# Graph attention with layer norm: the group's loads issued in pieces, slot by slot, two groups ahead

## The chip, the cores and the metric

The kernel runs on one core of a Trainium2 chip. The metric is device time in microseconds (us) of one execution; lower is better. A core has five engines that run their own lists of instructions and wait for each other by semaphores: TensorE (PE in the profile; PEld are its weight loads), VectorE (DVE), ScalarE (ACT), GpSimd (POOL) and SyncE (SP). SP computes nothing here: it issues plain loads and stores. POOL issues the indirect gathers. All transfers run on the core's 16 DMA engines.

## What is computed

One graph layer on 6250 nodes of 128 numbers and 206250 edges, sorted by receiver, then a residual and a layer norm:

```python
w_ij = silu(edge_feats @ rad_W1 + rad_b1) @ rad_W2 + rad_b2
w_ij = w_ij + (silu(chi_scalar @ sph_W1 + sph_b1) @ sph_W2 + sph_b2)
q_i = (x @ Wq)[receivers]          # 8 heads of 16
k_j = (x @ Wk)[senders]
v_j = (x @ Wv)[senders]
alpha = (q_i * w_ij * k_j).sum(-1) / sqrt(16) * cutoffs
out = segment_sum(alpha * v_j, receivers) / 16
x = layernorm(x + out)
```

Everything is float32. Each edge brings 32 + 32 features, a weight, a sender and a receiver.

## The kernel before

*Tiles.* 128 edges are a tile, 4 tiles (512 edges) a quad, 4 quads a group. There are 101 groups and 403 quads. A group's quads are taken in the order 0, 2, 1, 3; the place in this order is called the slot, so slots 0, 1, 2, 3 hold quads 0, 2, 1, 3. Quads of slots 0 and 1, and those of slots 2 and 3, form pairs for the features' first matmul.

*Start.* The first stage computes the keys and values of all nodes, stores them in a table in memory (kv_tab), turns the receivers into positions within a window of 32 rows per quad (rel, stored in memory as rel_lin), and makes tables of window starts (qb_i per quad, gb_i per group).

*The loop* runs over groups g and slots. The order of the work is written by hand (a manual schedule): each engine's list is the order in which the program calls. In a slot for quad q:

- `gathers` (L132): four indirect gathers on POOL, each 128 rows of 1 KB of kv_tab, for the quad 14 slots ahead, into a ring of 16 buffers named kv. A buffer comes free when VectorE's msg (L415) has read it.
- `weigh` (L375): two matmuls (L379), then ScalarE adds the bias and writes w (L381).
- `turn_back` (L395) of the quad before: four transposes of u into pu (L399).
- `take_q` (L384): receivers' queries spread to the edges by a matmul with hotT (L388).
- in slots 0 and 2 `hidden` (L359) for the next pair: four matmuls from feats (L367), each into one of four PSUM buffers named ph, and four silus on ScalarE (L372).
- in slot 1 `sum_group` of group g-2 (two matmuls, L446 and L448, and a copy to tot on ScalarE, L450) and `turn_q` of group g+1 (a transpose of xq, L336, and a copy, L338); in slot 3 `make_q` of group g+1.
- `sum_quads` of group g-1: matmuls that add messages per receiver (L425); two tiles' worth in slot 1, one each in slots 2 and 3.
- `scores` (m at L404, L406, L407), `multiply` (u at L393) and `messages` (msg at L415) on VectorE. m needs pu from TensorE and the gathered kv.
- in slot 2 the transposed one-hots hotT of group g+1 (L350, from relb) and `statistics` of group g-2, which needs xw; after every fourth group it also normalizes four groups' rows and stores them (L479).

*SP's list* in this order for group g: after slot 0, `load_q(g + 1)` (four loads of 32 rows of x at a start that SP reads from qb_i, 16 KB each, L158, tile xq), `load_xw(g - 1)` (64 KB, L455) and `load_rel(g + 1)` (four loads of 32 KB that copy a quad's receivers to 32 rows each, L150, tile relb); after slot 1, `load_feats(g + 2)` (one load of 128 rows of 4 KB, 512 KB, L140); in slot 2 of every fourth group four stores of 64 KB. SP works through its list as fast as waits allow: a load waits until its buffer is free (xq, relb, feats and xw have two buffers each), a store until ScalarE has written its rows. In feats, rows 0 to 63 hold quads 0 and 1 side by side, rows 64 to 127 quads 2 and 3.

Before the loop come, in this order, `turn_q(0)`, `make_q(0)`, the one-hots of group 0, `load_feats(1)`, `load_rel(1)` and `hidden` for the first pair.

Of the kernel before, what the change touches and what calls it, by code (L numbers as in the profile page):

```python
# [12 lines left out]
F32 = mybir.dt.float32  # L13
BF16 = mybir.dt.bfloat16
# [8 lines left out]
P = 128  # L23
N = 6250
D = 128
HEADS = 8
HD = D // HEADS
R = 32
# [3 lines left out]
NQ = GT // QT  # L32
NG = math.ceil(E / (P * GT))
NT = NG * GT
EG = P * GT
EQ = P * QT
# [15 lines left out]
def gnn_kernel(ctx, tc, x, src, dst, weight, edges, rad_W1, rad_b1, rad_W2, rad_b2,  # L52
# [12 lines left out]
    nc = tc.nc  # L65
# [13 lines left out]
    w1 = const.tile([P, D], F32, name="w1")  # L79
# [20 lines left out]
    gp = ctx.enter_context(tc.tile_pool(name="group", bufs=2))  # L100
# [15 lines left out]
    def start_of(table, i, last):  # L116
        return nc.values_load(table[:1, i:i + 1], engines=(SP,), min_val=0, max_val=last,
                              skip_runtime_bounds_check_because="the table is clamped to it")
# [10 lines left out]
    feats_of, relb_of, act_of, kv_of, hot_of, hotT_of, xq_of, q_of, msg_of = ({} for _ in range(9))  # L129
    po_of, part_of, to_of, tot_of, xw_of, y0_of, u_of = ({} for _ in range(7))  # L130

    def gathers(q):  # L132
        kv = quad_of("kv", RING, 2 * D)
        for t in range(QT):
            gather(kv[:, t, :], kv_tab, src_i[:, q * QT + t:q * QT + t + 1])
        kv_of[q] = kv

    def load_feats(g):
        feats_of[g] = gp.tile([P, EG // 2], F32, name="feats")
        nc.sync.dma_start(feats_of[g], edges[g])  # L140

    def quads_in(g):
        return min(NQ, QUADS - g * NQ)

    def load_rel(g):

        relb_of[g] = gp.tile([P, EQ], BF16, name="relb")
        for j in range(NQ):
            t = g * GT + j * QT
            nc.sync.dma_start(relb_of[g][j * W:(j + 1) * W, :],  # L150
                              rel_lin[t:t + QT, :].rearrange("t e -> (t e)").partition_broadcast(W))

    def load_q(g):

        xq_of[g] = gp.tile([P, D], F32, name="xq")
        for j in range(quads_in(g)):
            r = start_of(qb_i, g * NQ + j, N - W)
            nc.sync.dma_start(xq_of[g][j * W:(j + 1) * W, :], x[ds(r, W), :])  # L158

# [172 lines left out]
    with tc.tile_pool(name="ps", bufs=1, space=PSUM) as pp:  # L332
        def turn_q(g):
            n = quads_in(g) * W
            pt = pp.tile([P, EQ], F32, name="ph", bufs=4)
            nc.tensor.transpose(pt[:, :n], xq_of[g][:n, :], ident[:n, :n])  # L336
            xq_of[g] = gp.tile([P, P], F32, name="xqT")
            nc.scalar.activation(xq_of[g][:, :n], pt[:, :n], AF.Copy)  # L338
# [20 lines left out]
        def hidden(pair):  # L359

            for q in pair:
                g, j = divmod(q, NQ)
                r0, c0 = 2 * R * (j // 2), EQ * (j % 2)
                for i in range(2):
                    ph = pp.tile([P, EQ], F32, name="ph", bufs=4)
                    r = slice(r0 + i * R, r0 + (i + 1) * R)
                    nc.tensor.matmul(ph, w1[r, :], feats_of[g][r, c0:c0 + EQ], start=True, stop=True)  # L367
                    act_of[q, i] = ph
            for q in pair:
                for i in range(2):  # L370
                    act = ep.tile([P, EQ], F32, name="act", bufs=8)
                    nc.scalar.activation(act, act_of[q, i], AF.Silu, bias=b1[:, i:i + 1])  # L372
                    act_of[q, i] = act

        def weigh(q):  # L375

            pw = pp.tile([P, EQ], F32, name="ph", bufs=4)
            for i in range(2):
                nc.tensor.matmul(pw, w2[:, i, :], act_of[q, i], start=(i == 0), stop=(i == 1))  # L379
            w = ep.tile([P, EQ], F32, name="w")  # L380
            nc.scalar.activation(w, pw, AF.Identity, bias=bsum)  # L381
            return w

        def take_q(q):  # L384
            g, j = divmod(q, NQ)
            b = slice(j * W, (j + 1) * W)
            pq = pp.tile([P, EQ], F32, name="pq")
            nc.tensor.matmul(pq, q_of[g][b, :], hotT_of[g][b, :], start=True, stop=True)  # L388
            return pq
# [5 lines left out]
        def turn_back(q):  # L395

            pu = pp.tile([P, QT, D], F32, name="pu")
            for t in range(QT):
                nc.tensor.transpose(pu[:, t, :], u_of[q][:, t * P:(t + 1) * P], ident)  # L399
            return pu  # L400
# [37 lines left out]
        def part_sums(g):  # L438
            n = quads_in(g) * W
            part_of[g] = gp.tile([P, D], F32, name="part")  # L440
            nc.scalar.activation(part_of[g][:n, :], po_of[g][:n, :], AF.Copy)  # L441

        def sum_group(g):
            n, part, to = quads_in(g) * W, part_of[g], to_of[g]
            ph = pp.tile([P, EQ], F32, name="ph", bufs=4)
            nc.tensor.matmul(ph[:, :D], to[:n, 0, :], part[:n, :], start=True, stop=(g == 0))  # L446
            if g:
                nc.tensor.matmul(ph[:, :D], to[:, 1, :], tot_of[g - 1], start=False, stop=True)  # L448
            tot_of[g] = gp.tile([P, D], F32, name="tot")
            nc.scalar.activation(tot_of[g], ph[:, :D], AF.Copy)  # L450

        def load_xw(g):
            r = start_of(gb_i, g, N - P)
            xw_of[g] = gp.tile([P, D], F32, name="xw")
            nc.sync.dma_start(xw_of[g], x[ds(r, P), :])  # L455
# [40 lines left out]
        def verdict():  # L496

            pe = pp.tile([P, D], F32, name="po")
            nc.tensor.matmul(pe[:1, :8], ones[:, :1], ends, start=True, stop=True)
            found = gp.tile([1, 1], F32, name="found")  # L500
            nc.vector.tensor_reduce(found, pe[:1, :8], AX.X, OP.add)
            nc.vector.tensor_scalar(general, found, 0.0, None, op0=OP.is_gt)
# [3 lines left out]
        one_hots_T(0)  # L506
        one_hots(0)
        load_feats(1)
        load_rel(1)
        hidden(pairs[0])  # L510
        before = None
        for g in range(NG):
            last = g == NG - 1
            for slot, j in enumerate((0, 2, 1, 3)):
                q = g * NQ + j
                i = g * NQ + slot
                if q >= QUADS:
                    continue
                if i + AHEAD < len(order):
                    gathers(order[i + AHEAD])  # L520
                if slot == 0 and 2 <= g:
                    part_sums(g - 2)
                    if g == CHECK + len(checks) + 1:
                        verdict()
                w = weigh(q)
                if before is not None:
                    pu = turn_back(before)
                pq = take_q(q)
                if slot % 2 == 0:
                    u = 2 * g + slot // 2 + 1  # L530
                    if u < len(pairs):
                        hidden(pairs[u])
                if slot == 1 and 2 <= g:
                    sum_group(g - 2)
                if slot == 1 and g + 1 < NG:
                    turn_q(g + 1)
                if slot == 3:
                    make_q(g + 1)
                if 1 <= g:
                    for t in ((), (0, 1), (2, 3))[slot] if last else ((), (0, 1), (2,), (3,))[slot]:  # L540
                        sum_quads(g - 1, t)
                if before is not None:
                    alpha = scores(before, pu)
                multiply(q, pq, w)
                if before is not None:
                    messages(before, alpha)
                before = q
                if slot == 0:
                    if g + 1 < NG:
                        load_q(g + 1)  # L550
                    if 1 <= g:
                        load_xw(g - 1)
                        if g + 1 < NG:
                            load_rel(g + 1)
                if slot == 1:
                    if g + 2 < NG:
                        load_feats(g + 2)
                    if 1 <= g:
                        place(g - 1)
                    if last:  # L560
                        place(g)
                        load_xw(g)
                if slot == 2 and g + 1 < NG:
                    one_hots_T(g + 1)
                if slot == 2 and 2 <= g:
                    statistics(g - 2)
                if slot == 3:
                    one_hots(g + 1)
                    if CHECK <= g < CHECK + len(checks):
                        checks[g - CHECK]()  # L570
        g = NG - 1
# [170 lines left out]
```

## Time and profile before

| what | value |
|---|---|
| three runs | 2854.62, 2856.44, 2858.70 us |
| median | 2856.44 us |
| the profiled execution | 2843.93 us |
| its span, first to last instruction | 2841.9 us |
| mean granted TensorE clock | 0.847 |
| busy: PE, DVE, ACT, POOL | 81%, 50%, 35%, 54% of the span |
| gathers of kv on POOL | 1580 x 948 ns |
| moved by DMA | 310.42 MB, mean 109 GB/s |

The page cuts the span into 40 equal slices; a digit is the busy share of a slice in tenths (9 is 90% or more). PEclk is the clock that TensorE was granted, in tenths of full speed. A line of a group of instructions reads: line of the code, engine, operation, output and inputs, shapes, count, busy time in us and mean ns of one, then the idle time of the engine just before them and what ended it ("remote" is a releaser that the profile doesn't know, "issue" none that it shows). In a timeline the columns are start, us, engine, line, operation, and in brackets the idle time before it with its releaser. In a table of stretches each engine has its busy share of the stretch and, in brackets, the number of instructions.

### The profile page before, as it was taken

To read this page: it belongs to the slowest core of one execution; us is meant where nothing else is said; L and a number is where in the kernel's file an instruction comes from. 1 tells how busy PE (TensorE), PEld (TensorE's weight loads), DVE (VectorE), ACT (ScalarE), POOL (GpSimd) and SP (SyncE) were. 2 spreads that over 40 slices of the span, in tenths; PEclk is the share of its full clock that TensorE was granted. 3 is DMA by queue.
4 is the path that set the end of the run, shared out by engine and by line. 5 is a ranking of instruction groups with operands and counts; after the bars stand their busy time and mean duration, and the time that the engine had idled before them with its cause. 6 is when DMAs were issued, how large, how long until landed. Compare 5 with 4: busy or idle time off the path is not lost. (4 is left out here: it accounts for less than half of the span.)

```text
span 2841.9 us, 32012 instructions
## 1 busy us (share of the span) xinstructions
PE 2310.3 (81%) x9843; PEld 1023.9 (36%) x9843; DVE 1412.9 (50%) x2874; ACT 1000.3 (35%) x1826; POOL 1530.0 (54%) x1620
## 2 busy tenths in 40 slices
PE   5578878878887888888888888888888878788887
PEld 4333333333333333333333333333333333333333
DVE  3244554555554544545454454554544545455456
ACT  1233333333332433333333343333333333333334
POOL 4455555555555555555555555555555555555540
PEclk7788988888788887878888888888888888888889
DMA  5433333333333333333333333333334333333330
GB/s 175 133 111 97 118 105 114 113 102 111 118 105 111 102 118 102 110 111 104 110 107 112 116 98 110 119 102 120 108 99 119 103 106 116 107 112 113 108 99 26
DMA packets 166844, 310.42 MB, mean 109 GB/s; under 512 B 46530, under 2 KB 99212, under 8 KB 166668
## 3 DMA queue, kind: packets, MB, share of 16 engines
q0 software_dynamic: 76864, 209.29, 25.4%
q1 hardware_dynamic: 88316, 98.64, 10.5%
q8 instruction: 79, 1.29, 0.2%
q14 instruction: 97, 0.79, 0.1%
q10 hardware_dynamic: 1488, 0.40, 0.1%
HBM read 294.70 MB, written 13.46 MB: 108 GB/s over the span
## 5 line engine op out<-in xcount | busy, mean ns | idle before, releaser
L113 POOL DMA_INDIRECT kv<-kv_tab,src_i x1580 | 1498.5, 948 | 1217.7 <-DVE msg L415 748.5
L379 PE MATMUL ph<-act,w 128*128 128x512 f32 x1612 | 961.9, 726 | 95.8 <-ACT act L372 73.5
L404 DVE TENSOR_TENSOR m<-pu,kv 128x512 f32<-128x512 f32 x403 | 278.7, 691 | 1240.3 <-remote 434.1
L367 PE MATMUL ph<-feats,w 32*128 32x512 f32 x1612 | 626.3, 726 | 259.6 <-ACT w L381 198.4
L372 ACT ACTIVATE act<-ph,b 128x512 f32<-128x512 f32 x806 | 500.4, 688 | 317.6 <-PE ph L367 222.8
L381 ACT ACTIVATE w<-ph,bsum 128x512 f32<-128x512 f32 x403 | 276.9, 687 | 758.4 <-PE ph L379 286.7
L379 PEld LDWEIGHTS ph<-act,w 128*128 128x128 f32 x1612 | 325.1, 224 | 524.0 <-issue 367.4
L388 PE MATMUL pq<-hotT,q 32*128 32x512 f32 x806 | 475.8, 671 | 2.6 <-issue 2.6
L367 PEld LDWEIGHTS ph<-feats,w 32*128 32x128 f32 x1612 | 202.8, 206 | 454.9 <-ACT w L381 269.6
L399 PEld LDWEIGHTS pu<-ident,u 128*128 128x128 f32 x1612 | 215.1, 151 | 350.9 <-issue 200.6
L399 PE MATMUL pu<-ident,u 128*128 128x128 f32 x1612 | 259.5, 286 | 86.5 <-DVE u L393 83.7
L393 DVE TENSOR_TENSOR u<-pq,w 128x512 f32<-128x512 f32 x403 | 274.8, 682 | 55.1 <-PE ph L367 39.6
L406 DVE TENSOR_REDUCE side<-m 128x32 f32<-128x512 f32 x403 | 280.1, 695 | 13.7
L415 DVE TENSOR_TENSOR msg<-kv,side 128x512 f32<-128x512 f32 x403 | 273.0, 677 | 0.0
L425 PE MATMUL po<-msg,hot 128*32 128x128 f32 x3224 | 173.1, 312 | 2.9 <-ACT part L441 2.9
L450 ACT ACTIVATE tot<-ph 128x128 f32<-128x128 f32 x101 | 28.0, 277 | 399.3 <-remote 138.2
L388 PEld LDWEIGHTS pq<-hotT,q 32*128 32x128 f32 x806 | 123.2, 191 | 76.4 <-issue 76.4
L425 PEld LDWEIGHTS po<-msg,hot 128*32 128x32 f32 x3224 | 77.6, 117 | 154.2 <-issue 136.7
L407 DVE TENSOR_TENSOR side<-side,scale 128x32 f32<-128x32 f32 x403 | 80.4, 199 | 13.8
L346 ACT ACTIVATE q<-ph 128x128 f32<-128x128 f32 (+1 forms) x101 | 28.0, 277 | 144.8 <-issue 66.1
L350 DVE TENSOR_TENSOR hotT<-relb,side 128x512 f32<-128x512 bf16 x101 | 68.8, 681 | 0.0
L355 DVE TENSOR_TENSOR hot<-rel,side 128x512 f32<-128x512 f32 x101 | 68.8, 681 | 0.0
(83 smaller groups left out, 813.2 us busy)
## 6 DMA issues: line engine op xcount, KB each, us to landing
feats<-in_edges SPq DMA_DIRECT2D x101, 512.0 KB
kv<-kv_tab,src_i POOLq DMA_INDIRECT x1580
relb<-rel_lin SPq DMA_DIRECT2D x404, 32.0 KB
xw<-in_x SPq DMA_DIRECT2D x101, 64.0 KB
out<-y SPq DMA_DIRECT2D x101, 64.0 KB
xq<-in_x SPq DMA_DIRECT2D x403, 16.0 KB
kv_tab<-kv SPq DMA_DIRECT2D x12, 512.0 KB
act<-in_x SPq DMA_DIRECT2D x12, 256.0 KB
```

The source lines that it names most:

```text
L113: nc.gpsimd.indirect_dma_start(out=o, out_offset=None, in_=table, in_offset=bass.IndirectOffsetOnAxis(ap=index, axis=0))
L367: nc.tensor.matmul(ph, w1[r, :], feats_of[g][r, c0:c0 + EQ], start=True, stop=True)
L372: nc.scalar.activation(act, act_of[q, i], AF.Silu, bias=b1[:, i:i + 1])
L379: nc.tensor.matmul(pw, w2[:, i, :], act_of[q, i], start=(i == 0), stop=(i == 1))
L381: nc.scalar.activation(w, pw, AF.Identity, bias=bsum)
L388: nc.tensor.matmul(pq, q_of[g][b, :], hotT_of[g][b, :], start=True, stop=True)
L393: nc.vector.tensor_tensor(u_of[q], pq, w, op=OP.mult)
L399: nc.tensor.transpose(pu[:, t, :], u_of[q][:, t * P:(t + 1) * P], ident)
L404: nc.vector.tensor_tensor(m, pu, kv_of[q][:, :, :D], op=OP.mult)
L406: nc.vector.tensor_reduce(alpha, m.rearrange("p t (h e) -> p t h e", e=HD), AX.X, OP.add)
L415: nc.vector.tensor_tensor(msg_of[q].rearrange("p t (h e) -> p t h e", e=HD), kv_of[q][:, :, D:].rearrange("p t (h e) -> p t h e", e=HD), a ...
L425: nc.tensor.matmul(po_of[g][j * W:(j + 1) * W, :], hot_of[g][:, j * QT + t, :], msg_of[g * NQ + j][:, t, :], start=(t == 0), stop=(t == QT ...
```

## The change

The features' tile becomes two tiles, feats0 (quads 0 and 2) and feats1 (quads 1 and 3), each 128 rows of 2 KB with two buffers of its own, and each is loaded in two pieces of 64 rows and 128 KB: pieces 0 and 1 into feats0, 2 and 3 into feats1. After every slot of group g SP is given one piece of the features of group g+2, one load of 32 rows of x (xq) for it, and one quad's receivers (relb), where before it had four of a kind in one place: xq and relb were loaded one group ahead after slot 0, the features two groups ahead after slot 1. Tiles xq and relb get three buffers instead of two. `load_xw(g - 1)` stays after slot 0, now behind these three. `load_q(1)` moves ahead of the loop. The bytes loaded and all instructions of TensorE, VectorE, ScalarE and POOL, and their order, stay as they are.

```diff
--- before.py
+++ after.py
@@ -135,25 +135,34 @@
             gather(kv[:, t, :], kv_tab, src_i[:, q * QT + t:q * QT + t + 1])
         kv_of[q] = kv
 
-    def load_feats(g):
-        feats_of[g] = gp.tile([P, EG // 2], F32, name="feats")
-        nc.sync.dma_start(feats_of[g], edges[g])
+    def load_feats(g, parts=range(4)):
+
+
+        for k in parts:
+            i, b = k // 2, slice(k % 2 * 2 * R, (k % 2 + 1) * 2 * R)
+            if k % 2 == 0:
+                feats_of[g, i] = gp.tile([P, EQ], F32, name=f"feats{i}")
+            nc.sync.dma_start(feats_of[g, i][b, :], edges[g, b, i * EQ:(i + 1) * EQ])
 
     def quads_in(g):
         return min(NQ, QUADS - g * NQ)
 
-    def load_rel(g):
-
-        relb_of[g] = gp.tile([P, EQ], BF16, name="relb")
-        for j in range(NQ):
+    def load_rel(g, quads=range(NQ)):
+
+        for j in quads:
+            if j == 0:
+                relb_of[g] = gp.tile([P, EQ], BF16, name="relb", bufs=3)
             t = g * GT + j * QT
             nc.sync.dma_start(relb_of[g][j * W:(j + 1) * W, :],
                               rel_lin[t:t + QT, :].rearrange("t e -> (t e)").partition_broadcast(W))
 
-    def load_q(g):
-
-        xq_of[g] = gp.tile([P, D], F32, name="xq")
-        for j in range(quads_in(g)):
+    def load_q(g, quads=range(NQ)):
+
+        for j in quads:
+            if j >= quads_in(g):
+                continue
+            if j == 0:
+                xq_of[g] = gp.tile([P, D], F32, name="xq", bufs=3)
             r = start_of(qb_i, g * NQ + j, N - W)
             nc.sync.dma_start(xq_of[g][j * W:(j + 1) * W, :], x[ds(r, W), :])
 
@@ -360,11 +369,11 @@
 
             for q in pair:
                 g, j = divmod(q, NQ)
-                r0, c0 = 2 * R * (j // 2), EQ * (j % 2)
+                r0 = 2 * R * (j // 2)
                 for i in range(2):
                     ph = pp.tile([P, EQ], F32, name="ph", bufs=4)
                     r = slice(r0 + i * R, r0 + (i + 1) * R)
-                    nc.tensor.matmul(ph, w1[r, :], feats_of[g][r, c0:c0 + EQ], start=True, stop=True)
+                    nc.tensor.matmul(ph, w1[r, :], feats_of[g, j % 2][r, :], start=True, stop=True)
                     act_of[q, i] = ph
             for q in pair:
                 for i in range(2):
@@ -507,6 +516,7 @@
         one_hots(0)
         load_feats(1)
         load_rel(1)
+        load_q(1)
         hidden(pairs[0])
         before = None
         for g in range(NG):
@@ -545,16 +555,13 @@
                 if before is not None:
                     messages(before, alpha)
                 before = q
-                if slot == 0:
-                    if g + 1 < NG:
-                        load_q(g + 1)
-                    if 1 <= g:
-                        load_xw(g - 1)
-                        if g + 1 < NG:
-                            load_rel(g + 1)
+                if g + 2 < NG:
+                    load_feats(g + 2, (slot,))
+                    load_q(g + 2, (slot,))
+                    load_rel(g + 2, (slot,))
+                if slot == 0 and 1 <= g:
+                    load_xw(g - 1)
                 if slot == 1:
-                    if g + 2 < NG:
-                        load_feats(g + 2)
                     if 1 <= g:
                         place(g - 1)
                     if last:
```

## The prediction

> **What bounds the kernel now.** I read the page first (busy rows, clock row, costliest groups), then stretches of single groups, then the timeline of one group, then the waits of SP's queue and of TensorE.
>
> The page, parts 2 and 5:
>
> ```profile
> PE   5578878878887888888888888888888878788887
> POOL 4455555555555555555555555555555555555540
> PEclk7788988888788887878888888888888888888889
> ...
> L113 POOL DMA_INDIRECT kv<-kv_tab,src_i x1580 | 1498.5, 948 | 1217.7 <-DVE msg L415 748.5
> ...
> L404 DVE TENSOR_TENSOR m<-pu,kv 128x512 f32<-128x512 f32 x403 | 278.7, 691 | 1240.3 <-remote 434.1
> ```
>
> No engine is full: PE is at 81%, its granted clock at 0.85, and both POOL (waiting for VectorE's msg to free a kv buffer, 748.5 us) and VectorE (before m, 1240.3 us) stand idle for long. Four single groups by stretch, three with gathers and one after the last gather (columns: us, busy share with count of PE, PEld, DVE, ACT, POOL, then granted clock, DMA share, GB/s):
>
> ```profile
> 1405.10:1432.70 27.60, 22.99 (x96) 9.67 (x96) 13.47 (x27) 8.70 (x17) 15.17 (x16) 0.88 0.35 103
> ...
> 1487.80:1514.20 26.40, 23.21 (x96) 10.09 (x95) 13.44 (x28) 8.37 (x16) 14.94 (x16) 0.87 0.45 127
> 1189.80:1216.30 26.50, 22.21 (x96) 9.69 (x96) 13.36 (x27) 8.48 (x16) 14.80 (x17) 0.82 0.36 111
> ...
> 2779.80:2798.90 19.10, 18.08 (x96) 8.59 (x97) 13.49 (x28) 8.86 (x17) 0.00 (x0) 1.00 0.18 53
> ```
>
> The same 96 matmul records take 19.1 us without gathers and 26.4 to 27.6 us with them. From the starts of m, groups 0 to 96 average 27.08 us; sixteen gathers, one per 1.25 us, are 20.0 us of it. The rest is in the timeline of one such group:
>
> ```profile
> 1511.10 0.36 SPq L140 DMA_DIRECT2D feats<-in_edges  x1
> ...
> 1515.44 0.39 PE L448 MATMUL ph<-tot,to 128*128 128x128 f32 x2
> ...
> 1518.27 0.60 PE L399 MATMUL pu<-ident,u 128*128 128x128 f32 x4
> ...
> 1521.78 0.94 POOL L113 DMA_INDIRECT kv<-kv_tab,src_i  x1 [0.30 <-issue]
> 1523.70 0.28 ACT L450 ACTIVATE tot<-ph 128x128 f32<-128x128 f32 x1 [9.27 <-remote]
> ...
> 1525.35 0.69 DVE L404 TENSOR_TENSOR m<-pu,kv 128x512 f32<-128x512 f32 x1 [7.59 <-remote]
> ...
> 1528.46 0.94 POOL L113 DMA_INDIRECT kv<-kv_tab,src_i  x1 [5.73 <-DVE msg L415]
> ```
>
> The transposes that m waits for end at 1518.87, yet m starts 6.5 us later, and ScalarE's tot stands as long, 2.6 us after POOL's last gather ended (1522.73). POOL then idles 5.7 us until msg frees a buffer. I call this a stall: about one per group, and nearly every stall over 3 us ends only when POOL has run out of free buffers. Its cause is not named by the profile ("remote"). After it the granted clock reads 0.50 for some 6 us, and the next slot takes 7.0 us instead of 4.2. So a group costs POOL's 20 us plus POOL's idle time around one such run-out.
>
> SP's queue and TensorE, waits:
>
> ```profile
> SPq L140 <- PE ph L367: 493.8, 63, 18.2
> SPq L455 <- DVE st L465: 463.9, 66, 16.5
> SPq L479 <- ACT y L476: 443.6, 25, 21.7
> ...
> PE ph L336 <- issue: 21.5, 10, 7.3
> ...
> PE ph L336 <- DMA xq<-in_x: 7.0, 6, 1.9
> ```
>
> SP waits 1400 us on compute: its loads are early. The one place where compute waits for a load is L336, which needs xq.
>
> **The change part by part.** The order of the instructions on PE, VectorE, ScalarE and POOL is the same before and after; only SP's list differs.
>
> *Features in four pieces.* Three issues more per group; one takes 0.36 us (0.357 median of the 101), so 1.1 us per group on SP, which waits 1400/101 = 14 us per group: cost 0, and no compute engine waits for feats (no wait of L367 on a DMA is listed). If that cover were gone, 1.1 us per group would be 107 us. Transfer: the whole 512 KB showed as DMA share 0.76, 0.85, 1.00 in three 1 us slices (up to 391 GB/s); a 128 KB piece is bounded by that rate (0.33 us) and by the relb load's row (32 KB per 0.45 us of issue, so 1.8 us). Either lands far inside the more than one group by which it is early: 0.
>
> [...]
>
> *When the pieces go.* The first two (buffer feats0) wait for hidden of slot 2 a group earlier, the other two for hidden of slot 0; so SP sends two bursts per group, not four. Slot 0: from 512 + 4x16 KB to 256 + 32 + 64 = 352 KB. Slot 2: from xw 64 + relb 128 = 192 KB to 256 + 32 + 64 + 64 = 416 KB. Does this move the stall? In groups after the four output stores feats goes in slot 2 instead (1496.93 in the group that starts at 1487.8): that group is 26.4 us and the stall is still there, m starting at 1498.65 after 7.55 us idle. So the burst in slot 0 isn't what makes it. But its place does change: around 1190 m's gaps within a group are 5.1, 9.5, 3.4, 8.6 us, where the commoner form is 11.1, 7.0, 4.2, 5.1. Groups with a first gap of 10.8 us or more: 49, mean 28.1 us; the other 48: 26.0 us. They partly pay for each other (a short group follows a long one), so the whole 2.1 us is no gain per group. Any four groups in a row take 103.7 to 114.1 us, most of them 105.4 to 111.0, against the mean of 108.3: per group -0.7 to +0.7 us, over 97 groups -71 to +65 us. These are the bounds for a new phase of loads. I take -10 us, near the middle, a little below since the largest burst shrinks.
>
> *xq two groups ahead.* Gain: at most the waits of L336. Of 21.5 us, 7.3 lie at 112 us in the start; 14.2 + 7.0 = 21.2 us remain. But in the group at 1487.8 PE waited 1.5 us there and m came 9.88 us after L448 started, against 9.91 in the group of 1511.10, which did not wait: the stall hides it. Bounds -21 and 0; I take -5, nearer that pair.
>
> *relb per quad, two groups ahead.* hotT shows no idle time for relb, before or after: 0. Late next is nothing that SP loads: xw stays in its place behind a feature piece, and y's add waits for no DMA in the profile; the output stores now stand ahead of the fourth piece instead of the next xq, and this piece has a group to spare.
>
> *Start.* Features 0 in four issues put 1.1 us ahead of the last two kv_tab stores, and features 1 and xq 1 go out earlier than group 0 needs them. Bounds 0 and +2; I take +1.
>
> Sum: -10 - 5 + 1 = -14 us. The profiled execution took 2843.9 us (span 2841.9 and 2.0 around it) and becomes about 2830; the runs' median stands 12.5 us above it, so 2856.4 becomes 2842.
>
> **The rivals.**
> 1. *A second stall per group (slower).* The burst in slot 2 grows from 192 to 416 KB and lands while POOL has just restarted. For it: around 1190 a stall of 5 us begins within 1 us of the xw and relb loads of slot 2. Against it: in the group at 1487.8 feats, xq, xw and relb all went in slot 2, and the next gaps were 6.2, 4.2, 5.1 us. Price: POOL's idle 5.7 us per added stall. It decides from the fourth extra stall on (14 us of gain used up at the third); in every tenth group 9 x 5.7 = 51 us, 2893; in every fifth 19 x 5.7 = 108 us, 2950.
> 2. *The loads settle into the better pattern everywhere (faster).* For it: four-group stretches at 105.4 us exist in the run. Against it: they never last. 71 us: 2785.
> 3. *The stall goes (much faster).* Then 20.0 us of POOL remain per group, 97 x 7.08 = 687 us: 2170. Against it: the stall is there in groups without feats in slot 0, and the gathers stay.
> 4. *The change does nothing that counts.* The loads were early before: 2856.
>
> **How the numbers follow.** The likeliest case (0.42) gives 2842, its own range 2815 to 2865. Rival 1: 0.33; rival 2: 0.15; rival 3: 0.03; rival 4: 0.07. The likeliest, 2842 within bounds of -71 and +65 us, gives 2770 to 2907; the upper end moves to 2920, to take in most of the first rival, and 0.1 lies above it. About 0.08 lies below 2770. This kernel's measurement tells 0.2% from no change, 5.7 us. Faster: 0.30 of the likeliest, 0.15 and 0.03: 0.48. Same: 0.05 of the likeliest and 0.06 of rival 4: 0.11. Slower: 0.33, 0.07 and 0.01: 0.41.
>
> **What would show it.** Right: L336 without waits for xq; feats as four issues in two pairs per group; stretches near 27 us with sixteen gathers; POOL's wait for msg near 748 us. Wrong: POOL's wait for msg well above 850 us (more stalls) or below 650; a wait of L367 on a feature DMA; single groups beyond 28 us as the rule. The number fails if the stall answers to SP's bursts in a way that no group of this run shows.

## The result, and the profile after

The changed kernel took 2862.83 us (median of 20 runs, 2847.96 to 2870.84) beside 2855.20 us (20 runs, 2848.66 to 2861.37) of the kernel before on the same chip: ratio 1.0019, 95% interval 1.0010 to 1.0028. That is 0.2% slower (0.27% between the medians), on the edge of what a measurement of this kernel can tell from no change. The forecast was 0.5% faster. On another chip the same change was later 2.0% faster; this decides how the forecast is to be read and is told below.

The profiled execution of the changed kernel took 2868.33 us, near the top of its runs, and that of before 2843.93 us, below all 20 runs of the comparison. The two profiles lie 24 us apart where the medians lie 7.6 us apart, so small differences between them are to be read with care.

The page of the changed kernel, busy tenths and the two groups that were shown of before:

```profile
PE   5678887888878788888788888887888878788788
POOL 4455555555555555555555555555555555555540
PEclk7678878889888898898888988988889889888899
...
L113 POOL DMA_INDIRECT kv<-kv_tab,src_i x1580 | 1493.6, 945 | 1247.1 <-DVE msg L424 784.2
...
L413 DVE TENSOR_TENSOR m<-pu,kv 128x512 f32<-128x512 f32 x403 | 278.5, 691 | 1273.8 <-remote 637.6
```

Nothing became full or empty. POOL's wait for msg is 784.2 us (748.5 before), m's wait that ends on an unknown releaser 637.6 us (434.1). Four groups by stretch (us; busy and count of PE, PEld, DVE, ACT, POOL; granted clock; DMA share; GB/s), the last without gathers:

```profile
1201.40:1228.60 27.20, 22.30 (x96) 9.53 (x96) 13.44 (x27) 8.64 (x17) 15.12 (x16) 0.87 0.36 108
1419.80:1447.30 27.50, 22.76 (x96) 9.75 (x97) 13.45 (x28) 8.92 (x17) 15.30 (x17) 0.88 0.36 107
1502.50:1529.00 26.50, 21.94 (x95) 9.43 (x95) 13.48 (x28) 8.46 (x16) 14.34 (x16) 0.87 0.43 125
2804.50:2823.10 18.60, 17.82 (x96) 8.45 (x97) 13.44 (x28) 8.67 (x17) 0.00 (x0) 1.00 0.15 46
```

The stall is still there, in the same place: in 93 of the 97 groups (87 before) VectorE stands idle and m starts over 3 us after the last transpose has ended. The timeline of a group that starts at 1228.64:

```profile
1232.73 0.60 PE L408 MATMUL pu<-ident,u 128*128 128x128 f32 x4
...
1236.21 0.95 POOL L113 DMA_INDIRECT kv<-kv_tab,src_i  x1 [0.30 <-issue]
1239.63 0.69 ACT L390 ACTIVATE w<-ph,bsum 128x512 f32<-128x512 f32 x1 [4.79 <-remote]
1239.69 0.69 DVE L413 TENSOR_TENSOR m<-pu,kv 128x512 f32<-128x512 f32 x1 [7.69 <-remote]
...
1242.79 0.94 POOL L113 DMA_INDIRECT kv<-kv_tab,src_i  x1 [5.63 <-DVE msg L424]
```

The transposes end at 1233.33, m starts 6.4 us later, after POOL's last gather has ended (1237.16), and POOL then waits 5.63 us for msg. From the starts of m, groups 0 to 96 average 27.33 us (27.08 before). The form with gaps of 11.0, 7.0, 4.2 and 5.1 us between the m's of a group, which was the commoner one before, now holds two thirds of the groups: 66 of 97 have a first gap of 10.8 us or more (49 before), and so have 37 of the 43 groups from 27 to 69. 0.26 us x 97 = 25 us is the whole distance of the two spans.

The waits of SP's queue and of TensorE:

```profile
SPq L145 <- PE ph L376: 979.2, 124, 12.9
SPq L488 <- ACT y L485: 407.0, 24, 18.0
...
SPq L464 <- DVE st L474: 36.1, 3, 18.0
```

```profile
PE ph L345 <- issue: 5.7, 1, 5.7
```

The features' pieces wait for hidden in two pairs per group (124 waits). The transpose of xq (L345) waits once, in the start, and nowhere in the loop.

### The profile page after: what moved, and what is told of

Same layout as the page of the kernel before. It is cut to its first block, busy times and chain, and to the rows that moved or that the text cites. A ratio compares the mean times of both kernels' runs of the same rounds, so it can differ in the third digit from the quotient of the medians.

```text
span 2866.2 us, 32442 instructions
## 1 busy us (share of the span) xinstructions
PE 2307.5 (81%) x9843; PEld 1018.6 (36%) x9843; DVE 1412.1 (49%) x2874; ACT 1001.0 (35%) x1826; POOL 1524.9 (53%) x1620
## 3 DMA queue, kind: packets, MB, share of 16 engines
q0 software_dynamic: 76864, 209.29, 25.2%
## 4 chain that ended last, share of the span: by engine, by line
PE 61%; another core or an unknown queue 17%; issue 8%; ACT 6%; POOL 4%; DVE 3%; DMA 0%; DVEq 0%; SPq 0%; POOLq 0%; ACTq 0%
PE ph L388 25%; PE ph L376 11%; PE pq L397 10%; PE pu L408 5%; POOL kv L113 4%; PE po L434 4%; ACT act L381 3%; ACT w L390 2%; PE ph L353 1%; PE ph L455 1%; PE pk L228 1%; DVE side L415 1%; DVE m L413 1%; PE ph L457 1%
## 5 line engine op out<-in xcount | busy, mean ns | idle before, releaser
L113 POOL DMA_INDIRECT kv<-kv_tab,src_i x1580 | 1493.6, 945 | 1247.1 <-DVE msg L424 784.2
L388 PE MATMUL ph<-act,w 128*128 128x512 f32 x1612 | 937.9, 711 | 95.0 <-ACT act L381 88.0
L376 PE MATMUL ph<-feats,w 32*128 32x512 f32 x1612 | 664.3, 706 | 365.9 <-ACT w L390 288.0
L413 DVE TENSOR_TENSOR m<-pu,kv 128x512 f32<-128x512 f32 x403 | 278.5, 691 | 1273.8 <-remote 637.6
L397 PE MATMUL pq<-hotT,q 32*128 32x512 f32 x806 | 461.7, 653 | 0.3 <-issue 0.3
L376 PEld LDWEIGHTS ph<-feats,w 32*128 32x128 f32 x1612 | 210.3, 201 | 583.4 <-ACT w L390 376.3
L408 PEld LDWEIGHTS pu<-ident,u 128*128 128x128 f32 x1612 | 208.0, 146 | 284.4 <-issue 190.0
L408 PE MATMUL pu<-ident,u 128*128 128x128 f32 x1612 | 249.6, 279 | 38.9 <-DVE u L402 38.9
L359 DVE TENSOR_TENSOR hotT<-relb,side 128x512 f32<-128x512 bf16 x101 | 68.5, 678 | 0.0
L364 DVE TENSOR_TENSOR hot<-rel,side 128x512 f32<-128x512 f32 x101 | 68.5, 678 | 0.0
```

Source lines behind the costliest of these rows:

```text
L113: nc.gpsimd.indirect_dma_start(out=o, out_offset=None, in_=table, in_offset=bass.IndirectOffsetOnAxis(ap=index, axis=0))
L376: nc.tensor.matmul(ph, w1[r, :], feats_of[g, j % 2][r, :], start=True, stop=True)
L413: nc.vector.tensor_tensor(m, pu, kv_of[q][:, :, :D], op=OP.mult)
```

## Experiments on the chip of the first kind

Four theories stood against each other. A: the stall belongs to the gathers and the compute; what SP loads has next to no price. B: loads of 64 rows or their phase cost something. C: the place of xq and relb in SP's list is what counts. D: SP's loads make the stall. Four altered kernels were measured beside before, which had a median of 2850.88 us there (23 runs).

**The features alone.** xq and relb stay as before.

```diff
                 before = q
+                if g + 2 < NG:
+                    load_feats(g + 2, (slot,))
                 if slot == 0:
...
                 if slot == 1:
-                    if g + 2 < NG:
-                        load_feats(g + 2)
                     if 1 <= g:
```

(and load_feats and hidden as in the change)

> Kernel before with one part of the change: the features in four pieces of 64 rows, one issued after each slot, two groups ahead; xq and relb loaded as before. Theory A (the stall of each group belongs to gathers and compute; SP's loads don't shape it, and the change only alters how often a group falls into the commoner form with the long first gap): within 0.3% of before, groups near 27.1 to 27.3 us, the count of groups with a first gap of 10.8 us or more anywhere between 49 and 66. Theory B (the small loss comes from the pieces of 64 rows, which occupy the DMA engines longer): slower than before by 0.2% or more, like the whole change. Theory C (the loss comes from where the loads of receivers and x stand): same as before within 0.1%.

Measured: 2897.79 us, ratio 1.0169 (1.0127 to 1.0212). Its waits at TensorE:

```profile
PE ph L339 <- DMA xq<-in_x: 47.3, 13, 6.6
...
PE ph L339 <- issue: 18.0, 6, 6.4
```

Theory A (within 0.3%) and theory C (within 0.1%) missed this; B (0.2% or more) holds by the number, but not by its cause. All the waits in the loop lie in the group after the four output stores, so in every fourth. The timeline before the longest of them:

```profile
1506.99 7.94 SPq L482 DMA_DIRECT2D out<-y  x4
1514.98 1.12 SPq L143 DMA_DIRECT2D feats<-in_edges  x2
1517.16 7.87 SPq L161 DMA_DIRECT2D xq<-in_x  x4
...
1525.88 0.45 PE L339 MATMUL ph<-ident,xq 128*128 128x128 f32 x1 [6.60 <-DMA xq<-in_x]
```

In SP's list two feature pieces now stand between the stores and `load_q(g + 1)`. In none of the 24 such places does a piece wait for its buffer by more than 0.02 us; their two issues alone move the first xq load from 0.50 to 1.83 us after the last store (medians). The four loads of xq then take 5.7 us here (4.3 before), 2.8 us in the kernel without gathers below, so they come late, by up to 6.6 us. With 3.2 us behind an output store the waits at TensorE are 68.5 us, 40 us more than the 28.5 us of before, and the time rose by 47 us. Single groups reach 34.3 us.

**xq and relb alone.** The features stay whole.

```diff
-                if slot == 0:
-                    if g + 1 < NG:
-                        load_q(g + 1)
-                    if 1 <= g:
-                        load_xw(g - 1)
-                        if g + 1 < NG:
-                            load_rel(g + 1)
+                if g + 2 < NG:
+                    load_q(g + 2, (slot,))
+                    load_rel(g + 2, (slot,))
+                if slot == 0 and 1 <= g:
+                    load_xw(g - 1)
```

(and load_q, load_rel and the early load_q(1) as in the change)

> Kernel before with the other part of the change: xq and relb two groups ahead, one quad's after each slot, three buffers; the features in one load of 512 KB as before. Theory A: within 0.3% of before; TensorE's waits for xq before L336 in the loop (21 us) are gone, and the time hardly moves, since the stall covers them. Theory B (loss from the 64-row pieces): same as before or faster by up to 0.3%. Theory C (loss from xq and relb): slower by 0.2% or more.

Measured: 2853.47 us, ratio 1.0007 (0.9984 to 1.0031). The waits for xq in the loop are gone, and the time is the same: those of before, 21 us in the loop, some 1.4 us each, lay under the stall. The mean group of its profile is 27.16 us, 52 groups have the long first gap. So with xq far ahead the pieces cost next to nothing (1.0019 with them, 1.0007 without), and without it they cost 1.7%: in this change the second part pays for the first.

**No loads of features, relb or xq in the loop.** From group 2 on the tiles of groups 0 and 1 are used again: the kernel leaves out the loads of all later groups.

```diff
                     if g + 1 < NG:
-                        load_q(g + 1)
+                        xq_of[g + 1] = xq_raw[(g + 1) % 2]
+                        relb_of[g + 1] = relb_of[(g + 1) % 2]
...
                     if g + 2 < NG:
-                        load_feats(g + 2)
+                        feats_of[g + 2] = feats_of[g % 2]
```

(load_rel(g + 1) goes too, and load_q(1) stands ahead of the loop)

> Kernel before without SP's loads of features, receivers and rows of x from group 2 on: every later group reuses the tiles of groups 0 and 1 (this leaves out those loads, so it computes with other edges' data). Gathers, xw and the stores stay. Theory A (stall made by gathers and compute): groups still 26.5 to 27.4 us, the stall stays, time within 2% of before. Theory D (SP's loads make or lengthen the stall, and the change failed because its bursts are as bad): groups fall to 20 to 24 us, time 2200 to 2550 us.

Measured: 2858.49 us, ratio 1.0034 (1.0012 to 1.0055). The page:

```profile
L113 POOL DMA_INDIRECT kv<-kv_tab,src_i x1580 | 1497.3, 948 | 1240.9 <-DVE msg L415 778.2
...
L404 DVE TENSOR_TENSOR m<-pu,kv 128x512 f32<-128x512 f32 x403 | 278.7, 691 | 1279.0 <-remote 702.9
```

The stall is there without the loads: theory D falls. And a kernel that loads nothing is as slow as the changed one: 27.26 us per group, the long first gap in 75 groups, m's unknown wait 702.9 us. So the 0.2% need not be a price of the new loads. What fits is that the loads of before, xq above all, now and then pushed a group out of its commonest form, and the mean over the forms was a little shorter; over the profiles of before, xq and relb alone, the changed kernel and no loads the count of long first gaps is 49, 52, 66 and 75 and the span 2841.9, 2853.0, 2866.2 and 2864.5 us. The features alone do not fit in this row: 8 long first gaps and 2900.0 us, with the waits for xq on top. These are single executions, and the intervals of the ratios overlap; this reading is argued, not shown.

**No gathers after the first fourteen quads.** Scores and messages go on with the rows of those quads.

```diff
-                    gathers(order[i + AHEAD])
+                    kv_of[order[i + AHEAD]] = kv_of[order[(i + AHEAD) % AHEAD]]
```

> Kernel before without gathers after the first 14 quads: later quads reuse the first 14 buffers of keys and values (this leaves out the gathers, so it computes with other edges' keys and values). All of SP's loads stay as before. Theory A: no stall, groups near 19 us as in groups 97 to 99 of the profile before, about 134 + 101 x 19 = 2050 us. Theory D: stalls remain beside the loads, groups of 23 us or more, above 2400 us.

Measured: 2064.62 us, ratio 0.7249 (0.7211 to 0.7286), 19.07 us per group. The page:

```profile
PE   4779999999999999999999999999999999999996
...
PEclk7889999999999999999999999999999999999998
...
L404 DVE TENSOR_TENSOR m<-pu,kv 128x512 f32<-128x512 f32 x403 | 278.1, 690 | 471.0 <-PE pu L399 470.9
```

m now waits for TensorE's transposes and for nothing unknown. On this chip there is no stall without the gathers.

Does m wait for gathered rows in the stall? The semaphores and DMA packets in the trace of before say no. In the group of the prediction's timeline m waits for one semaphore, which TensorE alone raises; a rise is on record at 1525.32 us and m starts at 1525.35. By then the rows of its quad and of the next 60 gathers had landed. Of m's waits over 3 us, 61 end on an unknown releaser: TensorE's semaphore is in all of them and alone in 53, and in each at least 53 later gathers had landed when the wait began. So what comes late is TensorE's signal, or the result behind it: a matmul's end is modelled in the profile, which cannot part the two. SP is slowed as well. The 1216 short register instructions between its loads and stores take 0.03 to 0.04 us at the median, but 163 of them take 0.5 us or more in before, against none in the kernel without gathers.

## The same kernels on another chip

The later runs were made on another chip. There before takes 2088 to 2094 us (medians of 17, 13, 12 and 8 runs in four sets), with all its gathers, and no wait in its profile ends on an unknown releaser. Whether that is the chip itself or its condition on that day, no run tells.

**Before and the changed kernel there.**

> The changed kernel once more, beside the kernel before. Theory A (the loads have no price, the stall decides): as in the first comparison, ratio 1.000 to 1.003, mean group 27.1 to 27.4 us, and the first gap of 10.8 us or more in 50 to 75 of 97 groups: that count differs from execution to execution of one kernel. Theory B (the pieces or their phase cost something): the ratio is clearly above 1.002 and the count of groups with that first gap stays near 66.

> The kernel before, for its profile beside the other runs of this call. There are two kinds of chip so far: one where before takes 2850 us with a stall in each group, and one where it takes 2088 us and the changed kernel's groups have no stall. On the second kind before should show 19.8 us per group, PE over 90% busy, and 40 to 60 us of waits of the transpose of xq for its load (L336), which the changed kernel has not. On the first kind: as before, 27.1 us per group, 7 us of such waits.

> The changed kernel once more. On the kind of chip with stalls (before 2850 us): 1.000 to 1.003, mean group 27.1 to 27.4 us. On the kind without (before 2090 us): 0.977 to 0.983, mean group 19.4 us.

Measured: the changed kernel 2045.58 us, ratio 0.9799 (0.9773 to 0.9826), and in a later set 2045.00 us, 0.9782 (0.9748 to 0.9815). So it is 2.0% faster; the first expectation missed this, having been written for the other kind of chip. The page of before on this chip:

```profile
PE   8999999998999989988998989989999889999997
...
PEclk9999999999999999999999999999999999999998
...
L113 POOL DMA_INDIRECT kv<-kv_tab,src_i x1580 | 1496.5, 947 | 489.8 <-issue 425.5
...
L404 DVE TENSOR_TENSOR m<-pu,kv 128x512 f32<-128x512 f32 x403 | 278.5, 691 | 555.5 <-PE pu L399 551.0
```

A gather takes 947 ns as on the other chip, but POOL hardly waits for msg (14.3 us), m waits for TensorE, and TensorE is 92% busy. What is late now shows in the waits at TensorE and in the timeline around one group that starts at 898.6:

```profile
PE ph L336 <- DMA xq<-in_x: 58.7, 23, 4.1
```

```profile
890.35 9.01 SPq L479 DMA_DIRECT2D out<-y  x4
899.86 2.82 SPq L158 DMA_DIRECT2D xq<-in_x  x4
...
899.89 0.39 PE L448 MATMUL ph<-tot,to 128*128 128x128 f32 x2
...
904.42 0.45 PE L336 MATMUL ph<-ident,xq 128*128 128x128 f32 x1 [4.14 <-DMA xq<-in_x]
```

In every fourth group SP stands at the output stores until 899.4; the four loads of xq for the next group come behind them, and the transpose that needs them in slot 1 of this very group waits 4.14 us. What this costs is in the stretches, before:

```profile
861.00:878.00 17.00, 16.22 (x90) 7.68 (x89) 13.10 (x27) 7.54 (x15) 13.04 (x14) 1.00 0.47 131
879.20:898.60 19.40, 18.09 (x97) 8.30 (x96) 13.86 (x29) 12.90 (x24) 14.53 (x17) 1.00 0.43 122
898.60:923.80 25.20, 20.28 (x96) 9.48 (x97) 13.51 (x28) 8.89 (x17) 19.11 (x21) 0.86 0.58 167
923.80:942.40 18.60, 17.82 (x96) 8.45 (x97) 13.44 (x28) 8.69 (x17) 14.03 (x16) 1.00 0.49 145
```

and after the change:

```profile
938.10:957.40 19.30, 18.04 (x96) 8.25 (x96) 13.82 (x29) 12.83 (x24) 14.72 (x16) 1.00 0.42 117
957.40:979.40 22.00, 19.51 (x96) 9.22 (x97) 13.49 (x28) 8.86 (x17) 16.52 (x19) 0.92 0.64 180
```

The group with the wait takes 25.2 us where its neighbour takes 18.6: 4.1 us of waiting, and 2.5 us more for the same matmuls, PE busy 20.28 us where it is 17.82, at a granted clock that falls to a mean of 0.86. Over the run (groups 2 to 96) such fourth groups average 22.98 us before and 20.45 after, 24 x 2.53 = 61 us gained; the other 71 are 0.18 us longer, 13 us given back. The difference, 48 us, is that of the two spans (2090.2 and 2043.3 us) to within about 1 us.

The 13 us given back are the next limit, POOL: the groups from 80 on have all of them. Its gathers come every 1.25 us in both kernels; its last one starts at 2028.6 us before and at 2024.2 after, and the kernel ends 62 us and 19 us later. In the profile of the changed kernel m waits 102.0 us for gathered rows (3.5 us before), and from group 80 on its groups take 20.0 us, sixteen gathers. The wait for xq isn't all gone either: one of its four loads still goes behind the stores, and L345 still has 22 us of idle time before it in all, which the profile puts down to tot (8.4 us) and to nothing that it shows (12.6 us).

**The parts there.** The same kernels as in the first set.

> The features' part alone, xq and relb as before. On the kind of chip without stalls: if the pieces are without a price and only push xq back in SP's list, the waits for xq grow to 100 to 200 us and the ratio is 1.02 to 1.08; if the gain on that chip comes from the pieces, 0.98. On the kind with stalls: 1.013 to 1.021 as measured there.

> xq and relb two groups ahead, features whole. On the kind of chip without stalls: if the gain is the waits for xq, 0.975 to 0.985, all of the changed kernel's gain; if the gain needs the pieces too, 0.99 to 1.00. On the kind with stalls: 0.998 to 1.003 as measured there.

Measured: the features alone 1.0139 (1.0095 to 1.0184), xq and relb alone 0.9798 (0.9759 to 0.9837). The waits at TensorE of the two:

```profile
PE ph L339 <- DMA xq<-in_x: 81.7, 23, 5.4
```

```profile
PE ph L340 <- DMA xq<-in_x: 2.6, 2, 1.9
```

All of the gain is xq; the pieces alone add 23 us of the same wait and lose 25 us. The loss was under the expected 1.02, since the waits grew to 82 us and not to 100 or more.

**Features in two loads of 128 rows.** As the changed kernel, but each of the two tiles in one load.

```diff
             if k % 2 == 0:
                 feats_of[g, i] = gp.tile([P, EQ], F32, name=f"feats{i}")
-            nc.sync.dma_start(feats_of[g, i][b, :], edges[g, b, i * EQ:(i + 1) * EQ])
+                nc.sync.dma_start(feats_of[g, i], edges[g, :, i * EQ:(i + 1) * EQ])
```

> The changed kernel, but each of the tiles feats0 and feats1 is loaded by one load of 128 rows and 256 KB in place of two of 64 rows and 128 KB. Theory A: the same as the changed kernel, 1.000 to 1.003 of before. [...]

Measured: 2047.46 us beside 2045.58 us of the changed kernel in the same set; against before 0.9803 (0.9776 to 0.9829) and 0.9799. The 64 rows cost the kernel nothing here. By the DMA packets in the traces, a piece of 64 rows takes 1.05 us from first to last packet and a load of 128 rows 1.57 us (medians), so two pieces, one after the other, take 2.1 us for the same bytes. The transfer does not lie on the path: the matmuls that read the features (L376) have 0.0 us of idle time before them in the profile of either kernel.

**The changed kernel without gathers.** The edit is that of the kernel without gathers above, made in the changed kernel.

> The changed kernel without the gathers after the first fourteen quads (scores and messages go on with the rows of those quads). If its loads have no price, the groups are those of TensorE's work alone, 18.5 to 19.1 us on either kind of chip, 1990 to 2060 us; if the 64-row loads or their phase still cost something without gathers, longer than the 19.05 us of the kernel before without gathers.

Measured: 1981.37 us, 0.9470 of before (0.9432 to 0.9508), 18.82 us per group, PE at 94%. So the loads cost next to nothing against TensorE's own work, and the gathers are worth 64 us to the changed kernel on this chip, where on the other they are worth 786 us to before.

**Gathers that nobody reads, and pauses between gathers.** These were made to find the cause of the stall. In the first the later gathers go to a ring of four buffers of their own, and the ring that is read has 12 buffers; in the second POOL writes a small tile after each gather.

```diff
-                    gathers(order[i + AHEAD])
+                    gathers(order[i + AHEAD], "spare_kv", 4)
+                    kv_of[order[i + AHEAD]] = kv_of[order[(i + AHEAD) % AHEAD]]
```

```diff
             gather(kv[:, t, :], kv_tab, src_i[:, q * QT + t:q * QT + t + 1])
+            nc.gpsimd.memset(pause[:, :96], 0.0)
```

> The kernel before with all gathers after the first ten quads sent to a ring of four buffers that nobody reads; scores and messages use the rows of the first ten quads (their gathered rows are left out), and the ring that is read has 12 buffers. POOL no longer waits for VectorE, so the gathers run without a break for some 1975 us (1580 x 1.25) and then end. Theory A1 (the stall is interference: signals to VectorE and ScalarE come late while POOL's gathers run, and only its run-outs end it): groups while gathers run are longer than 27 us, and stand still for long stretches; after the gathers' end 19.1 us. Theory A2 (m waits for gathered rows that come late): 19 to 20 us per group from the start, 2050 to 2100 us in all.

> The kernel before with all gathers after the first ten quads sent to a ring of four buffers that nobody reads; scores and messages use the rows of the first ten quads (their gathered rows are left out), and the ring that is read has 12 buffers. On the kind of chip with stalls: theory A1 (signals to VectorE and ScalarE come late while gathers run) gives groups longer than 27 us as long as gathers run, and 19 us once they have ended; theory A2 (m waits for gathered rows) gives 19 to 20 us from the start. On the kind without stalls: as measured there, ratio 0.997 to 1.003.

> The kernel before with a memset of 128x96 on POOL after each gather, so that POOL's chain of gathers has a break of some 0.1 to 0.3 us after each. Theory A1 in the form that any break lets the late signals through: no stalls, groups paced by POOL at 16 x 1.35 to 1.55 us = 22 to 25 us, 2350 to 2650 us. Theory A1 in the form that only an end of the gathers does (POOL out of buffers): the stalls stay and each group grows by the 16 memsets, 2 to 5 us, 3050 to 3350 us. Theory A2: the rows come later still, so no gain, 2860 to 3350 us.

> A memset of 128x96 on POOL after each gather, 0.195 us as measured on the chip without stalls. On the kind of chip with stalls: theory A1 with any break enough gives no stall and 20.5 to 23.5 us per group, 2150 to 2450 us; A1 with only the run-out of POOL enough gives 27.1 + 16 x 0.2 = 30.3 us per group, 3160 us; A2 gives no gain, 2850 to 3200 us. On the kind without stalls: 1.027 to 1.035 again.

Neither ever ran on a chip with stalls, so on the stall they are inconclusive. Unread gathers: 0.9996, 0.9979, 0.9988 and 1.0010 of before in four sets; on this chip before is bound neither by gathered rows nor by POOL's buffers. Pauses: 1.0308, 1.0278 and 1.0288 in three sets; the first expectation, 2350 us and more, was far off: it was worked out for the chip with stalls, at 1.35 to 1.55 us per gather. From the page of the second of them:

```profile
L114 POOL DMA_INDIRECT kv<-kv_tab,src_i x1580 | 1506.8, 954 | 275.3 <-issue 254.1
...
L406 DVE TENSOR_TENSOR m<-pu,kv 128x512 f32<-128x512 f32 x403 | 278.5, 691 | 633.2 <-DMA kv<-kv_tab,src_i 294.8
...
L137 POOL MEMSET pause<- 128x96 f32 x1580 | 307.8, 195 | 1.1
```

308 us of work on POOL cost 57 to 65 us: POOL had slack until its chain, (1506.8 + 275.3 + 307.8) / 1580 = 1.32 us per gather, became the longest, and m then waits for rows.

## Why the prediction was wrong

- **The step that failed: the new phase of loads, -10 us.** It was the largest term, a guess between -71 and +65 us, taken below zero because the largest burst shrinks. On the chip of the forecast the whole change gave +7.6 us between the medians, and taking all these loads away gave as much (1.0034). The bursts of SP have no price there that a smaller burst could lower. The groups did settle into one form, but into the longer one: the table of four-group stretches in the prediction said which forms there are, and not which one an undisturbed kernel takes. The kernel without loads takes the form 11.0, 7.0, 4.2, 5.1 in most groups; that this is why the changed kernel does so too is argued, as said above.
- **xq two groups ahead, -5 us (bounds -21 and 0).** The bound 0 was right on that chip: 1.0007 alone. The prediction had the row for it, two groups with and without the wait whose m came equally late, and then took a quarter of the way to the other end. On the chip without stalls the same edit is worth 43 us, twice the lower bound, since the waits are 58.7 us there, and the group with one that was read above also ran at a granted clock of 0.86 where its neighbours had 1.00.
- **Features in four pieces, 0.** Right as far as issues, rows and transfers go (2047.46 us with two loads of 128 rows beside 2045.58; 1.0034 with no loads at all). But the sum missed that the pieces stand between the output stores and xq in SP's list: alone they cost 1.7% and 1.4%. The prediction called SP's list early by 14 us per group and did not ask where it is not early, behind the stores of every fourth group; in the change as made xq is far enough ahead for it not to matter.
- **relb 0, start +1.** No run speaks against either: the first m starts at 134.0 us before and 133.8 us after.
- **Rival 1, a second stall per group:** refuted for this chip; POOL's wait for msg went from 748 to 784 us, inside 650 to 850, not beyond. **Rival 2, the better pattern everywhere:** the pattern did settle, the other way. **Rival 3, the stall goes:** not through this change; the 2170 us worked out for it lies 80 us above what before takes where there is no stall. **Rival 4, the change does nothing that counts:** nearest to what happened on the chip of the forecast, with 0.07 the chance given to it was too low for a change to loads that were early.
- **What would show it:** L336 without waits for xq in the loop, features in two pairs, stretches near 27 us, POOL's wait near 748 us all came. They show that the mechanism of the group was understood; none of them could tell -14 from +8 us.

What stays open is the stall itself: TensorE's results are used 6.5 us late though the gathered rows are there, it needs the gathers, it needs none of SP's loads, and on another chip the same gathers at the same pace do not make it. Whether the work of POOL or the gathers' transfers hold the signals up, no run tells. Why the changed kernel is 0.2% slower and not just as fast is open too.

## What to carry to other kernels

A load that is moved ahead is worth what its wait costs outside any longer wait: read whether the consumer would have started earlier, in two groups with and without the wait, and then believe the answer (here 1.0007 for 21 us of waits that lay under the stall, 0.9798 for 58.7 us with no stall over them). In an in-order queue ask of each new load what stands behind it, even if it never waits itself: here two issues, 1.1 us, were enough; the xq loads that were due within the same group and stood behind the stores made TensorE wait 4.1 us in the group that was read. And a gain that is hidden under a stall on one chip can be the whole difference on another: before calling a change worthless, ask whether the thing that hides it is the kernel's or the machine's.

## What the runs showed of the hardware that was not expected

- The same program takes 2855 us on one chip and 2090 us on another, 37% more, while a gather takes 948 and 947 ns, m 691 ns and the transpose of xq 273 ns at the median on both. What differs in the profiles is the waits that end on an unknown releaser (434.1 us before m, and none), the granted clock (0.85 and 0.97) and SP's register instructions (163 of 1216 take 0.5 us or more, and none).
- Where gathers ran on the slower chip, m started over 3 us after TensorE's last transpose, with VectorE idle, in 87 of the 97 groups of before and 93 of the changed kernel (6.4 and 6.3 us at the median); in the group of the prediction's timeline the rows of its quad and of the next 60 gathers had landed by then, and ScalarE's tot came late as well, after 9.27 us idle. Without gathers that chip took 2065 us.
- On the faster chip one wait of 4.1 us at TensorE made its group 6.6 us longer; the granted clock of the group fell from 1.00 to 0.86.
- The features' transfers in 64 rows or 128 rows: 2045.58 and 2047.46 us, 0.1% apart, though two pieces, one after the other, take 2 x 1.05 = 2.1 us where one load took 1.57 us.
